# Linear attention with experts on one Trainium2 core: queries and keys by two levels of Strassen's algorithm, attention stages among their products

## The chip, the cores and the metric

The kernel runs on one core of a Trainium2 chip. The metric is the time of one execution on the device in microseconds; lower is better. The core has a matrix engine (TensorE, PE in the profile; its weight loads are PEld), a vector engine (VectorE, DVE), an engine for activations and copies (ScalarE, ACT), a general engine (GpSimd, POOL) and a queue that issues the DMAs (SyncE, SP). Each engine runs its instructions in the order in which they stand; a wait at the head of an engine holds everything behind it.

## What is computed

One layer, all of it in float32, on 1024 tokens (2 batches of 512) of width 512. The tokens are normalised; 32 heads of width 128 do linear attention with a decay per head, in blocks; the result is gated, normalised and projected back; a router with 8 experts of rank 16 and a base matrix are added.

```python
xn  = layernorm(x)
qkv = silu(xn @ qkv_w.T)                       # 32 heads x (q, k, v) x 128
for each block:                                # state kv: 128x128 per head and batch
    scores = (q @ k.T) * diag_decay
    out    = scores @ v + (q * q_decay) @ kv
    kv     = kv * block_decay + (k * k_decay).T @ v
gate = sigmoid(xn @ gate_w.T)
attn = gate * (norm_w * rms_normalised(out)) @ out_w.T
ffn  = xn @ W_base.T + b_base + sum over the top 2 of 8 experts of B_e (A_e xn) * 2 * weight
return x + attn + ffn
```

## The kernel before

**Setup.** The eight tiles of 128 tokens are loaded, normalised and transposed to xnT (one tile for each batch). The router's and the experts' first products (ra) and the base product (seeded banks, sent to DRAM as x_base) follow. The four blocks of xnT (feature half by batch) and their Strassen sums xsum are the outer level's seven operands xo[1..7]; for each, four inner sums xt[q] are made.

**Values and gates, two levels of Strassen's algorithm** (Winograd's form, seven products in place of eight, at each level). There are eight sets: values and gates of eight heads each, in turn. A set is seven rounds, one for each outer product q; a round is seven inner products of two matmuls with 256 columns (inner_product, L304 for values, L307 for gates). GpSimd prepares the weights' sums two rounds ahead (encode, L178 the outer and L192 to L195 the inner sums). The sums of products are made partly in PSUM: SLOTS gives the order of a round, (0,1), (0,5), (0,2), (1,7), (0,6), (0,3), (1,4), where the first number says whether the product belongs to this round or to the one before. Product 1 goes to bank pa; ScalarE copies pa to pb (L368) while product 5 runs; product 2 is added onto pa; product 6 onto pb; ScalarE copies pb to pd (L375); products 7 and 4 are added onto pd, 3 onto pc. VectorE takes y from pc and w from pb (L361) and adds the rest (L342, L346, L354). The outer level's sums x1, u2, u3, u4 are kept in SBUF (sum, 4 buffers). The round q=7 gives two outer results and so has the most vector work. pa and pc come from three "fr" banks, pb and pd from four seeded banks. Results pass through silu or tanh (L320, L322) and go to DRAM (v_kept, gate_kept). Routing (route, transpose_experts) stands among the first rounds.

**Queries, keys and attention.** Then the pools change. For each head a unit makes q and k for both batches with one level: seven products of two matmuls with 512 columns (product, L482), with the sums of the weights on GpSimd (load_unit, L127 to L130), sums of products on VectorE (L497) and silu on ScalarE (L493); four "ch" banks. Between the products of pair p+1 stand the attention stages of pair p. An item is one head and batch, 64 in all. Its stages (attend): k is transposed in squares of 32 on VectorE (L543) and goes to DRAM and back as kt (L545, L550); scores (8 instructions on TensorE) and their mask (L558), qd on GpSimd (L561); kd on ScalarE from kt (L566); the blocks' states (6 instructions) and their recurrence on VectorE (L574, L576); the output pa (14 instructions), its square sq on ScalarE (L589) added to ssq on GpSimd (L590), and gT on VectorE (L592), which goes to DRAM (g_kept). Attention has two "sc" and two "at" banks. The experts' second products stand in the same loop (experts, eight times). From the last two pairs on, the out weights (load_out_w, scaled on ScalarE, L636) and the first gated inputs are loaded, and twelve early out products stand between the last attention stages.

**Out projection.** One level of Strassen over token half f and head pair p (out_product, L666, 256 columns); operands are summed on VectorE (L647 to L650) and GpSimd (L654 to L657); the results are scaled, added to x_back and stored.

The order on each engine is made by a scheduler from the order of the program and a model of readiness; buffers are given out from each pool's free slots.

Of the kernel before, what the change touches and what calls it, by code (L numbers as in the profile page):

```python
# [22 lines left out]

# [12 lines left out]
ALU = mybir.AluOpType  # L36
# [23 lines left out]
def attn_moe_kernel(ctx: ExitStack, tc: tile.TileContext, x, qk_w, v_w, gate_w, out_w, norm_w,  # L60
                    decay, base_w, base_b, router_a_w, lora_b, out):
    nc = tc.nc

    def pool(name, space=None, bufs=1):
        kw = {"space": space} if space is not None else {}
        return ctx.enter_context(tc.tile_pool(name=name, bufs=bufs, **kw))

    keep = pool("keep")
    dram = pool("dram", DRAM)
    wts = pool("wts")  # L70
    phase_a = ctx.enter_context(ExitStack())
    ps = phase_a.enter_context(tc.tile_pool(name="ps_a", bufs=1, space=PSUM))
    seeded = [ps.tile([P, 512], F32, tag=f"sd{i}", name=f"sd{i}") for i in range(4)]
    banks = {"fr": 3, "ra": 1}
# [3 lines left out]

    def mm(o, lhsT, rhs, start, stop):
        nc.tensor.matmul(o, lhsT, rhs, start=start, stop=stop)  # L80

# [4 lines left out]
    hT = keep.tile([P, NT, P], F32, tag="hT", name="hT")  # L86
    nw = keep.tile([P, H], F32, tag="nw", name="nw")
    xnT = [wts.tile([P, KC, S], F32, tag=f"xnT{b}", name=f"xnT{b}") for b in range(B)]
    xsum = [wts.tile([P, 2, S], F32, tag=f"xsum{i}", name=f"xsum{i}") for i in range(4)]
# [5 lines left out]
    x_kept, x_base = (dram.tile([P, NT, HID], F32, tag=n, name=n) for n in ("x_kept", "x_base"))  # L95

# [20 lines left out]
    units, masks = {}, {}  # L117
    wts_of = [wts, wts]

    def load_unit(i):  # L120

        where = wts_of[i // 2 % 2]
        w = where.tile([P, 2, KC, P], F32, tag="w", name="w", bufs=2)
        nc.sync.dma_start(w, qk_w[i])
        s = where.tile([P, 4, 2, P], F32, tag="ws", name="ws", bufs=2)
        a11, a12, a21, a22 = w[:, 0, 0:2], w[:, 0, 2:4], w[:, 1, 0:2], w[:, 1, 2:4]
        nc.gpsimd.tensor_tensor(s[:, 0], a21, a22, ALU.add)  # L127
        nc.gpsimd.tensor_tensor(s[:, 1], s[:, 0], a11, ALU.subtract)
        nc.gpsimd.tensor_tensor(s[:, 2], a11, a21, ALU.subtract)
        nc.gpsimd.tensor_tensor(s[:, 3], a12, s[:, 1], ALU.subtract)  # L130
        units[i] = w, s

    def load_pair(p):

        if p >= NP:
            return
        for j in range(2):
            m = wts.tile([P, 2, P], F32, tag="mask", name="mask", bufs=4)

            nc.sync.dma_start(m[:, 0, :], decay[2 * p + j][:, :P])  # L140
            nc.sync.dma_start(m[:, 1, :], decay[2 * p + j][P - 1, P : 2 * P].partition_broadcast(P))
            masks[2 * p + j] = m

    aw = phase_a.enter_context(tc.tile_pool(name="aw", bufs=1))
    NSET = 2 * (NG // 2)
    raws, sums2, operand = {}, {}, {}

    def load_set(n):  # L150
        s_, kind = divmod(n, 2)
        r = raws[n] = aw.tile([P, 2, HG * KC * P], F32, tag="raw", name="raw", bufs=2)
        for u in range(2):
            if kind == 0:
                nc.sync.dma_start(r[:, u].rearrange("p (k f) -> p k f", k=KC), v_w[2 * s_ + u])
            else:
                for f in range(HG):
                    nc.sync.dma_start(r[:, u, f * KC * P : (f + 1) * KC * P].rearrange("p (k d) -> p k d", k=KC),
                                      gate_w[8 * s_ + 4 * u + f])

    def raw_block(n, fo, ko):


        if n % 2 == 0:
            v = raws[n].rearrange("p u (ko ki fo y) -> p u ko ki fo y", ko=2, ki=2, fo=2)
            return v[:, :, ko, :, fo, :]
        v = raws[n].rearrange("p u (fo fi ko y) -> p u fo fi ko y", fo=2, fi=2, ko=2)
        return v[:, :, fo, :, ko, :]

    def inner(n, block, fi, ki):  # L170
        x_, y_ = (ki, fi) if n % 2 == 0 else (fi, ki)
        return block[:, :, x_, y_ * P : (y_ + 1) * P]

    def encode(n, q):

        def outer(k, a, b, op):
            t = sums2[n, k] = aw.tile([P, 2, 2, 256], F32, tag="s", name="s", bufs=4)
            nc.gpsimd.tensor_tensor(t, a, b, op)  # L178

        if q == 6:  # L180
            outer(1, raw_block(n, 1, 0), raw_block(n, 1, 1), ALU.add)
            outer(2, sums2[n, 1], raw_block(n, 0, 0), ALU.subtract)
        elif q == 7:
            outer(3, raw_block(n, 0, 0), raw_block(n, 1, 0), ALU.subtract)
        elif q == 3:
            outer(4, raw_block(n, 0, 1), sums2[n, 2], ALU.subtract)
        block = {1: lambda: raw_block(n, 0, 0), 2: lambda: raw_block(n, 0, 1), 3: lambda: sums2[n, 4],
                 4: lambda: raw_block(n, 1, 1), 5: lambda: sums2[n, 1], 6: lambda: sums2[n, 2],
                 7: lambda: sums2[n, 3]}[q]()
# [9 lines left out]
    for n in range(NSET):  # L199
        start = {0: [(0, 1), (1, 1), (0, 6)], 1: [(1, 6), (0, 4)]}.get(n, [(n, 1), (n - 1, 4), (n, 6)])  # L200
        rounds += start + [(n, q) for q in (2, 5, 7, 3)]
# [3 lines left out]
    lg = aw.tile([P, NT, NE], F32, tag="lg", name="lg")  # L205
    hl = aw.tile([P, NT, NE, R], F32, tag="hl", name="hl")
    xt = [aw.tile([P, 4, S // 2], F32, tag=f"xt{q}", name=f"xt{q}") for q in range(1, 8)]
    with tc.tile_pool(name="setup", bufs=1) as sp:
# [5 lines left out]
        for t in range(NT):  # L214
            nc.sync.dma_start(x_sb[t], x[t * P : (t + 1) * P, :])
            if t == 2:
                nc.sync.dma_start(wra, router_a_w)
        nc.sync.dma_start(wbase, base_w)
        load_set(0)
        nc.sync.dma_start(nw, norm_w)  # L220
        load_set(1)
# [4 lines left out]
        def base(t):  # L226

            b, tt = divmod(t, TB)
            bp = seeded[t % 4]
            for c in range(KC):  # L230
                mm(bp, xnT[b][:, c, tt * P : (tt + 1) * P], wbase[:, c, :], c == 0, c == KC - 1)
            o = sp.tile([P, HID], F32, tag="based", name="based", bufs=3)
            nc.scalar.copy(o, bp)
            nc.sync.dma_start(x_base[:, t, :], o)


        stats = sp.tile([P, NT, 6], F32, tag="stats", name="stats")
        mv = sp.tile([P, NT, 2], F32, tag="mv", name="mv")
        for g, ts in enumerate(((0,), (1, 2), (3, 4, 5), (6, 7))):
# [4 lines left out]
            for i, t in enumerate(ts):  # L244
                b, tt = divmod(t, TB)
                xn = sp.tile([P, HID], F32, tag="xn", name="xn", bufs=4)
# [3 lines left out]
                for c in range(KC):  # L250
                    nc.tensor.transpose(tp[:, c * P : (c + 1) * P], xn[:, c * P : (c + 1) * P], ident)
                nc.scalar.copy(xnT[b][:, :, tt * P : (tt + 1) * P],
                               tp.rearrange("p (c s) -> p c s", c=KC))
                ra = bank("ra")
                for c in range(KC):
                    mm(ra[:, : NE + ER], xnT[b][:, c, tt * P : (tt + 1) * P], wra[:, c, :],
                       c == 0, c == KC - 1)
                nc.scalar.copy(lg[:, t, :], ra[:, :NE])
# [17 lines left out]
        for t in range(NT):  # L276
            base(t)
# [565 lines left out]
```

## Time and profile before

| what | value |
|---|---|
| median of 3 runs | 1201.85 us (1201.69 to 1202.39) |
| the profiled execution: time, span | 1200.23 us, 1198.4 us |
| granted TensorE clock | 1.0 in all slices |
| setup and base products | 0 to 52 us, TensorE busy 42.0 us |
| values and gates | 52 to about 405 us |
| queries, keys, attention | about 407 to 1009 us |
| out projection | about 1009 to 1198 us |
| L482, both operands from sums | x384, mean of one 593 ns, busy 179.9 us |
| L307 sd<-xt,e | x224, mean of one 379 ns, busy 55.0 us |
| POOL L590 ssq, L561 qd | mean 1279 ns, 1009 ns |
| ACT L566 kd, L589 sq | mean 612 ns, 593 ns |
| DVE L592 gT, L558 scores, L543 squares | mean 688 ns, 685 ns, 572 ns |
| DMA k_kept, kt, wo (time to landing) | 2.4 us, 2.7 us, 6.7 us |

How to read it: "busy" counts the time in which at least one instruction of the group runs. Matmuls overlap (the next one starts while the last still drains), so the mean of one is longer than its pitch. A matmul in float32 appears as two instructions. "Idle before, releaser" says what ended an engine's wait. The windows give the busy time of each engine in a stretch.

### The profile page before, as it was taken

Reading aid. Unit: us, or ns where it says so; the run is one execution under the profiler, and the core shown is the slowest. Engines: PE = TensorE matmul, PEld = TensorE weight load, DVE = VectorE, ACT = ScalarE, POOL = GpSimd, SP = SyncE. Lnnn points to the kernel's source line nnn. Section 1 sums busy time; section 2 is a strip of 40 time slices with the busy share of each in tenths; the row PEclk is TensorE's granted clock in tenths of the full one; section 3 lists DMA queues with packets and bytes.
Section 4 is the critical chain, followed back from the end, with each engine's and each line's share of the span. In section 5 each row is a group of like instructions: output and inputs, shape, how many; then the busy total and the mean of one; then the engine's idle time right before and its main releaser. Section 6 shows DMA issues by size and latency. Waiting matters only on the chain.

```text
span 1198.4 us, 15747 instructions
## 1 busy us (share of the span) xinstructions
PE 1179.0 (98%) x5352; PEld 863.1 (72%) x5352; DVE 660.0 (55%) x1158; ACT 375.2 (31%) x656; POOL 597.9 (50%) x670
## 2 busy tenths in 40 slices
PE   6999999999999999999999999999999999999998
PEld 5588888888888655666666666666666669888887
DVE  8777676675776544445445454444445644436334
ACT  3244444544444422232222223223222332310000
POOL 4547775766765233343443444344434344655552
PEclk9999999999999999999999999999999999999999
DMA  7214445244342555655565656655555655933221
GB/s 289 89 45 139 152 150 176 97 159 167 106 160 95 187 170 169 184 159 184 166 195 176 183 175 186 187 158 173 178 160 174 199 169 165 329 123 124 88 88 53
DMA packets 152240, 189.58 MB, mean 158 GB/s; under 512 B 47072, under 2 KB 114656, under 8 KB 150880
## 3 DMA queue, kind: packets, MB, share of 16 engines
q1 hardware_dynamic: 152160, 188.57, 49.5%
q8 instruction: 43, 0.70, 0.3%
q14 instruction: 37, 0.30, 0.1%
HBM read 119.31 MB, written 69.21 MB: 157 GB/s over the span
## 4 chain that ended last, share of the span: by engine, by line
PE 91%; DVE 6%; ACT 1%; issue 1%; DMA 0%; SPq 0%; DVEq 0%; ACTq 0%
PE ps_ch L482 32%; PE ps_ch L666 9%; PE ps_at L80 9%; PE ps_sc L80 8%; PE ps_fr L307 7%; PE ps_fr L304 6%; PE sd L307 5%; PE ps_sc L666 5%; PE sd L304 4%; PE ps_at L666 2%; PE sd L80 2%; DVE sum L346 2%; DVE z L346 2%; PE ps_ra L80 1%; DVE c L354 1%
## 5 line engine op out<-in xcount | busy, mean ns | idle before, releaser
L482 PE MATMUL ps_ch<-xsum,ws 128*128 128x512 f32 x384 | 179.9, 593 | 0.0
L561 POOL TENSOR_TENSOR qd<-q,mask 128x384 f32<-128x384 f32 x64 | 64.6, 1009 | 166.9 <-PE ps_at L80 166.9
L482 PE MATMUL ps_ch<-xnT,w 128*128 128x512 f32 x256 | 120.5, 593 | 0.8 <-DVE z L346 0.8
L482 PEld LDWEIGHTS ps_ch<-xsum,ws 128*128 128x128 f32 x384 | 68.3, 191 | 62.6 <-issue 62.2
L80 PEld LDWEIGHTS ps_at<-scores,v 128*128 128x128 f32 x512 | 77.4, 192 | 28.0 <-issue 25.8
L592 DVE SCALAR_TENSOR_TENSOR gT<-gate,ps_at 128x512 f32<-128x512 f32 x64 | 44.0, 688 | 95.6 <-ACT sq L589 89.9
L497 DVE TENSOR_TENSOR c<-ps_ch,u 128x512 f32<-128x512 f32 x96 | 66.4, 691 | 49.6 <-PE ps_ch L482 49.3
L127 POOL TENSOR_TENSOR ws<-w 128x256 f32<-128x256 f32 x32 | 23.6, 738 | 135.4 <-DMA w<-in_qk_w 129.2
L666 PE MATMUL ps_ch<-wsum,gsum 128*128 128x256 f32 x384 | 89.1, 379 | 0.0
L80 PE MATMUL ps_at<-scores,v 128*128 128x128 f32 x512 | 88.4, 275 | 0.0
L80 PEld LDWEIGHTS ps_sc<-q,k 128*128 128x128 f32 x512 | 67.2, 192 | 29.3 <-issue 29.2
L590 POOL TENSOR_TENSOR ssq<-ssq,sq 128x512 f32<-128x512 f32 x62 | 79.3, 1279 | 11.2 <-ACT sq L589 11.2
L666 PEld LDWEIGHTS ps_ch<-wsum,gsum 128*128 128x128 f32 x384 | 72.3, 190 | 9.5
L493 ACT ACTIVATE k<-c 128x512 f32<-128x512 f32 x64 | 40.3, 630 | 117.8 <-DVE c L497 117.8
L80 PE MATMUL ps_at<-qd,state 128*128 128x128 f32 x384 | 74.2, 275 | 0.0
L80 PEld LDWEIGHTS ps_sc<-v,kd 128*128 128x128 f32 x384 | 52.8, 191 | 28.4 <-issue 27.5
L654 POOL TENSOR_TENSOR wsum<-wo 128x256 f32<-128x256 f32 x32 | 25.0, 782 | 91.8 <-PE ps_ch L666 37.4
L647 DVE TENSOR_TENSOR gsum<-gated 128x256 f32<-128x256 f32 x32 | 16.8, 526 | 97.2 <-PE ps_sc L666 74.6
L482 PEld LDWEIGHTS ps_ch<-xnT,w 128*128 128x128 f32 x256 | 44.0, 191 | 33.7 <-issue 32.3
L80 PE MATMUL ps_sc<-q,k 128*128 128x128 f32 x512 | 67.5, 275 | 0.0
L589 ACT ACTIVATE sq<-ps_at 128x512 f32<-128x512 f32 x62 | 36.8, 593 | 91.0 <-PE ps_at L80 87.1
L566 ACT ACTIVATE kd<-kt,mask 128x384 f32<-128x384 f32 x64 | 39.2, 612 | 72.7 <-PE ps_sc L80 28.8
(224 smaller groups left out, 2551.1 us busy)
## 6 DMA issues: line engine op xcount, KB each, us to landing
w<-in_qk_w SPq DMA_DIRECT2D x32, 512.0 KB, 4.6
v_kept<-z SPq DMA_DIRECT2D x64, 256.0 KB, 2.4
gate_kept<-z SPq DMA_DIRECT2D x64, 256.0 KB, 2.4
v<-v_kept SPq DMA_DIRECT2D x64, 256.0 KB, 2.9
gate<-gate_kept SPq DMA_DIRECT2D x64, 256.0 KB, 2.9
g_kept<-gT SPq DMA_DIRECT2D x64, 256.0 KB, 3.2
gated<-g_kept SPq DMA_DIRECT2D x32, 512.0 KB, 3.8
k_kept<-squares SPq DMA_DIRECT2D x64, 192.0 KB, 2.4
```

Source lines behind the costliest of these rows:

```text
L80: nc.tensor.matmul(o, lhsT, rhs, start=start, stop=stop)
L304: nc.tensor.matmul(o.rearrange("p (g j d) -> p j g d", g=2, j=2)[:, u], x_[:, u * P : (u + 1) * P], a, start=first and u == 0, stop=True, ...
L307: nc.tensor.matmul(o[:, u * HB : (u + 1) * HB], a[:, u], x_, start=first and u == 0, stop=True, skip_group_check=True)
L346: nc.vector.tensor_tensor(o, v, outer_sums[n, src][:, ij], ALU.add)
L482: nc.tensor.matmul(o, a[:, c, :], b[:, c, :], start=first and c == 0, stop=c == 1, skip_group_check=True)
L493: nc.scalar.activation(to[n, b], c, AF.Silu)
L497: nc.vector.tensor_tensor(o, p, t, ALU.add)
L561: nc.gpsimd.tensor_tensor(qd, q[:, P:].rearrange("p (j n) -> p j n", j=TB - 1), mask[:, 1, :].unsqueeze(1).to_broadcast([P, TB - 1, P]), A ...
L566: nc.scalar.activation(kd.rearrange("p j (a d) -> p a j d", a=4), kt, AF.Copy, scale=mask[:, 0, P - 1 : P])
L590: nc.gpsimd.tensor_tensor(ssq[b], ssq[b], sq, ALU.add)
L592: nc.vector.scalar_tensor_tensor(gT, gate.pop((head, b)), 1.0, pa, ALU.add, ALU.mult)
L666: nc.tensor.matmul(sums[n][:, i * HO : (i + 1) * HO], l[:, i * P : (i + 1) * P], r, start=p == 0 and i == 0, stop=p == NP - 1, skip_group_ ...
```

## The change

Queries and keys become eight more sets of the same rounds as values and gates (kind 2; a set is four heads, its outer blocks are pairs of heads), each round again seven inner products with 256 columns. Their results stay in SBUF (ring "qk", four tiles of q and k of one item). When an item's q and k are complete, its attention begins: the transpose two slots later, kt six slots later, the other stages through a generator (stages) from which the loop takes one stage for each 49/24 slots. Items run in the order in which they are complete. What does not get a turn by the last round is done after it, with the early out products.

For this the pools are merged. Values and gates share the rings of the attention; weights come block by block (load_block, 5 tiles) in place of set by set; the sums have three buffers in place of four, u3 takes u2's place and the outer weight sum 4 takes 2's; PSUM is three seeded banks (pb always the first, pd the other two in turn), two "fr", two "sc" and one "at"; pa and pc share the two "fr" in the new sets, and pc has "sc" in the old ones. The router's result goes through DRAM (routed). The experts' products stand among the rounds of values and gates (from round 8, every third). Masks are loaded for each item in place of each head. The out weights of the first four pairs and the first three gated inputs are loaded when the rounds are over.

```diff
-    seeded = [ps.tile([P, 512], F32, tag=f"sd{i}", name=f"sd{i}") for i in range(4)]
-    banks = {"fr": 3, "ra": 1}
+    seeded = [ps.tile([P, 512], F32, tag=f"sd{i}", name=f"sd{i}") for i in range(3)]
+    banks = {"fr": 2, "sc": 2, "at": 1}
+    RING = {"qk": (2, 4), "v": (1, 5), "gate": (1, 4), "scores": (1, 3), "gT": (1, 2), "sq": (1, 1)}
...
-    NSET = 2 * (NG // 2)
+    VG = 2 * (NG // 2)
+    NSET = VG + NG
+    def kind(n):
+        return 2 if n >= VG else n % 2
+    def load_block(n, fo, ko):
+        t = blocks[n, fo, ko] = aw.tile([P, 2, 2, 256], F32, tag="raw", name="raw", bufs=5)
...
+    def place(n, fo, to, ij):
+        fi, ti = divmod(ij, 2)
+        if kind(n) < 2:
+            return ring("v")
+        item = 4 * (n - VG) + 2 * fo + fi, to
+        if item not in qk:
+            qk[item] = ring("qk", [P, 2, S])
+        return qk[item][:, :, ti * HB : (ti + 1) * HB]
...
+        elif ij in (1, 2):
+            complete((4 * (n - VG) + 2 * fo + fi, to))
...
         if i == 1:
-            st["pb"] = seed_bank()
+            st["pb"] = seeded[0]
             nc.scalar.copy(st["pb"], st["pa"])
...
-            st["pd"] = seed_bank()
+            st["pd"] = seeded[1 + r % 2]
...
+    def complete(item):
+        items.append(item)
+        g = running[len(items) - 1] = attend(*item)
+        ready[len(items) - 1] = now[0] + 4
+        later[now[0] + 2].append(g)
+        later[now[0] + 6].append(g)
...
+    def stages():
+        for i in range(ITEMS + 2):
+            if i < ITEMS:
+                while i not in ready or ready[i] > now[0]:
+                    yield None
+                next(running[i])
+            if 1 <= i <= ITEMS:
+                next(running[i - 1])
+            if i < ITEMS:
+                yield True
+            if 1 <= i <= ITEMS:
+                next(running[i - 1])
+                yield True
+            if i >= 2:
+                next(running[i - 2])
+                yield True
...
         if i in (1, 5):
-            st["pa" if i == 1 else "pc"] = bank("fr")
+            st["pa" if i == 1 else "pc"] = bank("fr" if kind(rounds[r][0]) == 2 or i == 1 else "sc")
         inner_product(...)
         after(r, i)
+        if items:
+            credit = min(credit + 24 / 49, 1.5)
+            if credit >= 1 and next(stage):
+                credit -= 1
...
-    def product(o, a, b, first):
-        for c in range(2):
-            nc.tensor.matmul(o, a[:, c, :], b[:, c, :], start=first and c == 0, stop=c == 1, ...)
-    def unit(n):
-        ...
-    def projections(p):
-        ...
...
+    for i in range(EARLY):
+        load_gated(0, i)
+        load_out_w(i)
+    load_out_w(EARLY)
+    left = 0
+    while True:
+        now[0] += 1
+        for g in later.pop(now[0], ()):
+            next(g)
+        s_ = next(stage, "end")
+        if s_ == "end":
+            break
+        if s_:
+            left += 1
+            if left == 3:
+                sums[0].update({1: bank("fr"), 6: bank("fr"), 5: seeded[0], 7: seeded[1]})
+                for i in range(EARLY):
+                    operands(0, i)
+            if left >= 5:
+                for e in [next(early, None)]:
+                    if e:
+                        out_product(0, *e, sums[0])
```

## The prediction

> **What bounds the kernel now.** I read the page's engine totals first, then its chain of waits, then the same chain in order of time.
>
> ```profile
> span 1198.4 us, 15747 instructions
> PE 1179.0 (98%) x5352; PEld 863.1 (72%) x5352; DVE 660.0 (55%) x1158; ACT 375.2 (31%) x656; POOL 597.9 (50%) x670
> ```
> ```profile
> 457.98 6.87 PE ps_ch L482 x16
> ...
> 1159.36 2.59 PE ps_ch L666 x12
> ...
> 1186.98 5.18 PE ps_sc L666 x24
> ```
>
> TensorE is busy 98% of the span and carries 91% of the chain; no other engine passes 55%. The chain gives the true pitch of a matmul (the group means overlap): 6.87/16 = 0.430 us with 512 columns, 5.18/24 = 0.2157 us with 256. So halving the columns halves the time, and a product of two levels pays nothing extra on TensorE. Each f32 product shows as two instructions.
>
> Next, how well each stage fills TensorE: the windows by stage, on five whole sets of values and gates (145.74 to 366.61), the change of stages, and the stage of queries, keys and attention.
>
> ```profile
> 145.74:366.61 220.87, 218.73 (x982) 182.49 (x981) 148.92 (x211) 100.44 (x180) 150.25 (x161) 1.00 0.43 143
> ...
> 398.00:410.00 12.00, 9.98 (x40) 7.08 (x39) 6.61 (x11) 5.92 (x10) 0.00 (x0) 1.00 0.65 205
> 410.00:984.00 574.00, 574.00 (x2561) 356.79 (x2560) 281.54 (x537) 169.79 (x284) 243.03 (x265) 1.00 0.58 177
> ```
>
> Columns after the length: busy time of PE, weight loads, DVE, ACT, POOL. One-level queries and keys run with no idle TensorE at all. The two-level rounds do not quite: a set of seven rounds takes 220.87/5 = 44.2 us, and its 7 x 28 instructions at 0.2157 us are 42.3. So the form that queries and keys now take loses 1.9 us a set. Where, the timeline shows, at the round q=7:
>
> ```profile
> 171.31 2.41 DVE L346 TENSOR_TENSOR sum<-c,sum 128x512 f32<-128x512 f32 x1
> 173.64 0.68 DVE L346 TENSOR_TENSOR z<-c,sum 128x512 f32<-128x512 f32 x1
> 174.24 0.68 DVE L361 TENSOR_TENSOR y<-ps_fr,sum 128x512 f32<-128x512 f32 x1
> ```
> ```profile
> 175.07 1.10 PE L304 MATMUL ps_fr<-e,xnT 128*128 128x256 f32 x4 [0.23 <-DVE y L361]
> ```
> ```profile
> 170.82 2.35 POOL L178 TENSOR_TENSOR s<-s,raw 128x1024 f32<-128x1024 f32 x1
> ```
>
> An add of two SBUF tiles that elsewhere takes 0.68 us takes 2.41 while GpSimd runs its 2.35 us add; VectorE falls behind, y comes late, TensorE waits.
>
> **The change, part by part.** *Products.* Out go 32 units of 14 products of 512 columns: 896 instructions x 0.430 = 385.3 us. In come 8 sets x 7 rounds x 14 products of 256 columns: 1568 x 0.2157 = 338.2. On the path: -47.1 us. The built order has the 784 added products of that form, so the change does what it says there. GpSimd loses the 128 adds of load_unit (0.74 us each) and gains the encoding, 30.05 us a set by the windows (150.25/5); VectorE and ScalarE trade the unit's adds and copies for a round's.
>
> *Loads of the other engines.* A set now goes with 8 items of attention. TensorE: an item is 28 instructions; the timeline has 8 of them in 0.89 us, 0.111 each, so 3.11 us, and a set is 42.3 + 24.9 = 67.2 us. VectorE: 148.92/5 = 29.8 us for the rounds, and per item gT 0.688, scores 0.685, transpose 0.572, state 0.278 + 2 x 0.285, together 2.79: 29.8 + 22.3 = 52.1 us (78%). GpSimd: 30.05 + 8 x (1.009 + 1.279) = 48.4 (72%). ScalarE: 100.44/5 + 8 x (0.612 + 0.593) = 29.7 (44%). None becomes the bound on average, so what costs is lateness inside a set.
>
> *Lateness of the rounds.* A round's copy pb<-pa (0.575 us) must finish while TensorE runs one slot (0.863 us). In half of the gaps an attention stage now stands between products, which lengthens the cover. But in the two rounds around q=7 VectorE has some 11.8 us of work without a break (170.1 to 181.9 in the trace); with 2 x 8/7 items it has 11.8 + 6.4 = 18.2 us in two rounds of 9.6, about no slack. The bounds: 0 if the attention hides everything, 5 us a set if the waits of gT for sq (89.9 us over 64 items, 1.4 each) are also paid for the 2.3 items in these rounds, 1.9 + 3.2. I take 1.9, the value of the same rounds in this trace.
>
> *A wait that moves.* ScalarE's kd waits for kt to come back from DRAM, by the waits:
>
> ```profile
> ACT kd L566 <- DMA kt<-k_kept: 24.8, 18, 3.2
> ...
> ACT kd L566 <- DMA mask<-in_decay: 12.2, 8, 2.1
> ACT kd L566 <- DMA w<-in_qk_w: 6.6, 3, 2.9
> ```
>
> These 43.6 us (0.68 an item) cost nothing now: behind kd stand silu and copies with four ch banks in reserve. Afterwards pb<-pa stands behind it, and the next product but one waits for that. The distance from the transpose to the loading of kt also falls, from one item (about 9.1 us) to four slots with half a stage each (4 x (0.863 + 0.53) = 5.6 us), against 2.4 us for the write and 2.7 for the read. Bounds: 0, or all 0.68 x 8 = 5.5 us a set. The urgent copy comes once in 9.6 us and 26 waits of 1.7 us stand over it a fifth of the time, so I take 0.6. Banks are scarcer too: pa and pc have two between them (before three for the rounds), attention's at one (before two). A bank's next use is at least two slots and a stage, 2.8 us, after its last, and its reader takes 0.69: 0.25 us a set, bounds 0 and 0.9 (one late reader of 0.69 and a slot's gap). Together 2.75 us a set, 22.0 us for eight.
>
> *The rule of the port.* That a VectorE add of two SBUF operands and a GpSimd add exclude each other is in the row of 2.41 us; its mean excess is (1.38 - 0.69) + (0.98 - 0.69) = 0.98 us for each of two pairs a set, which is already inside the 1.9. The Trainium skill, SBUF — State Buffer, section "Who interferes with whom", says that the later of the two is blocked for the whole of the other's instruction, and this speaks against the change, since qd and ssq add GpSimd reads there. By it, in the worst case, four adds a set each wait a whole 2.4 us, 9.6 us in place of 1.9 to 2.0: 62 us more in eight sets, and the sum would be near 1240; by the row it stays as above.
>
> *The seam and the end.* At 398 to 410 TensorE idles 2.0 us where the stages change; the rounds run through: -2.0. At the other end twelve of the 192 attention stages are left when the rounds run out (24 stages to 49 slots, starting three rounds late). The first four pairs of out weights and three of g are loaded only then, seven DMAs of 512 KB, where the kernel before spread them over two pairs of heads. In the built order 45 attention matmuls (10.0 us) stand after the last round, ahead of the first out product, which needs 6.7 us for the weight's landing and 0.71 for its scaling; after it each wsum takes GpSimd 4 x 0.77 us. Bounds: 0, or 11 us (3.67 MB at the 329 GB/s of the page's fastest slice); I take 3, since the weights' adds come about as fast as TensorE uses them.
>
> *Costed at nothing.* The trip of routing through DRAM and the blockwise loads of weights: hidden by the 26 us in which TensorE multiplies by wbase and by the two rounds of lead; uncovered, the trip costs 4.3 us (an x load's landing). The experts among the gates' rounds: 8 x 2.55 us more for GpSimd, which is busy 30 of 44 us there; uncovered up to 2.5 us each. Twice as many mask loads (SyncE's queue, ahead of kt): 0.77 us an item of issue on a queue whose waits are for free buffers. Out products after the stages: unchanged.
>
> Sum: -47.1 + 22.0 + 3.0 - 2.0 = -24.1 us on the profiled span of 1198.4, or 1174.3. The median of the runs shown is 1201.85, 3.45 above the span; less 24.1 it is **1178 us**.
>
> **The rivals.** *The attention hides the rounds' lateness* (1 us a set at most, 2 at the end): -47.1 + 8 + 2 - 2 = -39, **1163**. For it: idle-free TensorE from 410 to 984, where the attention already stands among products. Against: those had four banks and no copy on the path.
> *VectorE sets the pace of the heavy rounds*: 5 us a set, 40 + 3 - 2 - 47.1 = -6, **1196**. For it 18.2 us of work in 19.2; against, waits vanish when VectorE is the late one.
> *Slower: ScalarE blocked by kt.* If every item's kd waits the 1.7 us that 26 of 64 wait now, and half of it reaches TensorE through pb<-pa, that is 64 x 0.85 = 54 us: **1232**. It decides from 24.1/64 = 0.38 us an item beyond my sum. For it: the shorter distance, and one in-order queue. Against: kd still stands at least four slots behind kt.
>
> **How the numbers follow.** Forecast (1168 to 1190) 0.45; hidden 0.25; VectorE 0.15, of it 0.03 within 0.2% (2.4 us, about what a measurement here can tell from no change); ScalarE 0.15. So faster 0.82, same 0.03, slower 0.15. The range 1157 to 1203 leaves out the best of the second case and most of the last.
>
> **What would show it.** Right: about 67 + 3 us a set in the new stage, matmuls at 0.2157 us, short TensorE waits for y, z and pb<-pa near q=7. Hidden: sets of 68 us. VectorE: TensorE idle behind VectorE in the heavy rounds, VectorE gapless. ScalarE: kd waiting for kt, TensorE idle until pb<-pa just after. The end: how long TensorE idles before the first out product. The prediction is wrong if a set takes over 73 us or the first stage lengthens.

## The result, and the profile after

The changed kernel takes 1257.93 us (median of 4 runs, 1254.14 to 1264.23); the kernel before took 1201.77 us beside it. The ratio is 1.0473, 95% interval 1.043 to 1.0516: it is slower, where 1178 us was predicted. The profiled execution took 1264.23 us, with a span of 1262.4.

The page's engine totals and slices of the changed kernel:

```profile
span 1262.4 us, 17952 instructions
...
PE 1177.9 (93%) x6024; PEld 1004.1 (80%) x6024; DVE 768.2 (61%) x1334; ACT 439.7 (35%) x780; POOL 742.9 (59%) x798
...
PE   6999999999999999999999997988978967999998
...
PEclk9999999999999999999999997998988998999999
```

TensorE is no longer 98% busy. No engine has taken its place; the holes lie in slices 25 to 34, where the granted clock dips too. Those slices are the later sets of queries and keys. Windows on sets 10, 13 and 15 (counted from the first set of values; busy time of PE, weight loads, DVE, ACT, POOL, then the clock) show it:

```profile
542.00:610.00 68.00, 66.32 (x407) 59.99 (x407) 47.73 (x85) 28.38 (x51) 46.26 (x48) 1.00 0.60 177
752.00:839.00 87.00, 76.43 (x416) 65.32 (x415) 49.02 (x90) 29.47 (x52) 47.75 (x48) 0.90 0.45 135
925.00:1029.00 104.00, 87.52 (x507) 76.48 (x506) 59.78 (x115) 32.71 (x58) 48.31 (x49) 0.92 0.46 135
```

The first and the second do the same work: DVE 48 and 49 us, ACT 28 and 29, POOL 46 and 48. One takes 68 us and the other 87.

A ledger, read from the starts of the products; "lost" is a stretch less its matmuls at full pitch (0.430 us for 512 columns, 0.215 for 256, 0.111 for 128). Sets 0 to 7 are values and gates, 8 to 15 queries and keys; the tail runs from the last round to the first matmul on ones, which begins the out projection's final sums.

| us | before | after |
|---|---|---|
| to the first round | 51.8 | 52.8 |
| sets 0 to 7 | 45.9 43.5 44.1 44.1 44.2 44.1 44.2 44.7, sum 355.0 | 46.7 48.4 47.7 46.2 45.0 44.3 44.3 44.3, sum 366.8 |
| lost in them | 17.1 | 21.9 |
| sets 8 to 15 | | 53.3 69.2 68.3 68.2 73.9 86.8 86.1 103.5 |
| lost in them | | 1.6 2.2 2.8 4.2 8.8 20.9 19.1 27.1 |
| tail | | 47.8, lost 18.1 |
| queries, keys, attention in all: time, work, lost | 605.6, 604.3, 1.3 | 657.2, 552.1, 105.0 |
| out | 186.1 | 185.7 |

So the products' saving is there: TensorE has 52.2 us less to do in the second stage. But 105 us are lost in place of 1.3, and they grow from set to set. Sets 9 to 11 took 69.2, 68.3 and 68.2 us, what the prediction gave a set (67.2 + 2.75). From set 12 on it breaks down.

Where, the timeline in set 14 shows:

```profile
843.59 0.60 ACT L530 ACTIVATE sq<-ps_at 128x512 f32<-128x512 f32 x1 [5.29 <-PE ps_at L89]
...
844.26 1.27 POOL L531 TENSOR_TENSOR ssq<-ssq,sq 128x512 f32<-128x512 f32 x1 [5.46 <-ACT sq L530]
...
845.49 2.34 POOL L155 TENSOR_TENSOR s<-s,raw 128x1024 f32<-128x1024 f32 x1
...
847.79 0.99 POOL L499 TENSOR_TENSOR qd<-qk,mask 128x384 f32<-128x384 f32 x1
...
848.82 0.69 DVE L345 TENSOR_TENSOR qk<-sd,y 128x512 f32<-128x512 f32 x1 [3.91 <-POOL qd L499]
...
849.56 1.91 PE L293 MATMUL sd<-xt,s 128*128 128x256 f32 x4 [3.47 <-DVE qk L345]
...
852.23 0.63 ACT L318 ACTIVATE qk<-qk 128x512 f32<-128x512 f32 x1 [2.06 <-DVE qk L349]
852.77 0.58 ACT L378 COPY sd<-sd 128x512 f32<-128x512 f32 x1
...
853.40 2.08 PE L293 MATMUL sd<-xt,e 128*128 128x256 f32 x4 [1.93 <-ACT sd L378]
```

This is a chain through all four engines. ScalarE's square has waited 5.29 us for TensorE's output stage, and GpSimd stands 5.46 us in ssq, waiting for that square. Behind ssq stand an outer sum of the encoding and qd. qd is the last reader of a q/k tile, and the ring has four, so VectorE may not write the next q until qd is done (3.91 us); TensorE's product waits for that add (3.47 us). Four matmul instructions take about 1.03 us at full clock; here they take 1.91 and 2.08, at half. The second of them had waited for a copy on ScalarE, which stood behind a silu that waited 2.06 us for VectorE's next q/k add. The waits of the whole run (us in total, times, longest), first the longest of all, then one from ScalarE's list:

```profile
POOL ssq L531 <- ACT sq L530: 185.1, 47, 10.5
```
```profile
ACT kd L506 <- DMA kt<-k_kept: 3.6, 3, 1.9
```

The kernel before had 11.2 us of the first:

```profile
POOL ssq L590 <- ACT sq L589: 11.2, 9, 3.3
```

The second answers to the 24.8 us that kd waited for kt before: the rival that blamed kt is refuted.

The instructions on each engine are much the same in every set from 9 on, but their built order is not. TensorE's, one line a set, where a dot is a product, s a scores or states stage and each a one of the seven matmuls of an output stage:

```
set 9   ..s..aaaaaaa..s..s..aaaaaaa..s..s..aaaaaaa..s..s..aaaaaaa..s..s..aaaaaaa...s.s..aaaaaaa...s.s..aaaaaaa....s.s..aaaaaaa..s
set 11  ...s.aaaaaa.sa......ssaaaaaaa....s.aa.saaaaa....s.aa.saaaaa.....s.aaaaaasa......saaaasaaa........saaaasaaa......
set 13  aasaaa......saaaaaasa.....saaaa.aasa.......ssaaaaaaa....s.aasaaaa.a....s.aa.saaaa.a...s.aaaasaaa.....saaaaaasa........
```

In set 9 the stages are spread over the products as the loop issues them. From set 11 on the scheduler puts two or three side by side, with up to eight products without one. GpSimd's order changes likewise: in sets 9 to 11 encodings and attention's adds take turns, from set 12 on two encodings stand behind three pairs of qd and ssq.

### The profile page after: what moved, and what is told of

It reads as the page before. It is cut to its first block, busy times and chain, and to the rows that moved or that the text cites. A ratio compares the mean times of both kernels' runs of the same rounds, so it can differ in the third digit from the quotient of the medians.

```text
span 1262.4 us, 17952 instructions
## 1 busy us (share of the span) xinstructions
PE 1177.9 (93%) x6024; PEld 1004.1 (80%) x6024; DVE 768.2 (61%) x1334; ACT 439.7 (35%) x780; POOL 742.9 (59%) x798
## 4 chain that ended last, share of the span: by engine, by line
PE 65%; DVE 9%; POOL 6%; issue 4%; DMA 3%; ACT 2%; SPq 2%; DVEq 0%; ACTq 0%; POOLq 0%
PE ps_fr L293 15%; PE sd L293 12%; PE ps_at L89 6%; PE ps_sc L89 6%; PE sd L652 6%; PE ps_fr L652 4%; PE ps_sc L652 4%; PE sd L290 4%; PE ps_sc L293 3%; PE ps_fr L290 3%; PE ps_sc L290 2%; DVE sum L349 2%; DVE v L349 2%; DVE qk L349 2%; POOL s L155 1%
## 5 line engine op out<-in xcount | busy, mean ns | idle before, releaser
L293 PE MATMUL sd<-xt,e 128*128 128x256 f32 x672 | 172.3, 385 | 6.0 <-ACT sd L378 5.8
L293 PEld LDWEIGHTS sd<-xt,e 128*128 128x128 f32 x672 | 125.7, 193 | 24.6 <-ACT sd L378 9.2
L318 ACT ACTIVATE qk<-qk 128x512 f32<-128x512 f32 x128 | 80.5, 630 | 152.0 <-DVE qk L349 90.4
L170 POOL TENSOR_TENSOR e<-s 128x256 f32<-128x256 f32 x64 | 46.7, 730 | 95.4 <-PE sd L293 70.5
L293 PE MATMUL ps_fr<-xsum,s 128*128 128x256 f32 x288 | 81.9, 406 | 12.0 <-DVE qk L349 11.8
L371 ACT COPY sd<-ps_fr 128x512 f32<-128x512 f32 x112 | 64.3, 574 | 77.4 <-PE ps_fr L293 48.3
L378 ACT COPY sd<-sd 128x512 f32<-128x512 f32 x112 | 64.4, 575 | 64.1 <-PE sd L293 47.5
L155 POOL TENSOR_TENSOR s<-raw 128x1024 f32<-128x1024 f32 x32 | 77.6, 2425 | 11.8 <-DMA raw<-in_qk_w 5.2
L89 PE MATMUL ps_at<-qd,state 128*128 128x128 f32 x384 | 76.8, 282 | 7.3 <-DVE state L516 6.2
L89 PEld LDWEIGHTS ps_at<-scores,v 128*128 128x128 f32 x512 | 77.2, 197 | 6.8 <-issue 2.5
L293 PEld LDWEIGHTS ps_fr<-xsum,s 128*128 128x128 f32 x288 | 54.2, 200 | 27.5 <-DVE qk L349 11.8
L89 PEld LDWEIGHTS ps_at<-qd,state 128*128 128x128 f32 x384 | 61.5, 196 | 11.0 <-DVE state L516 7.2
L499 POOL TENSOR_TENSOR qd<-qk,mask 128x384 f32<-128x384 f32 x64 | 65.9, 1035 | 7.0 <-ACT qk L318 2.5
L89 PE MATMUL ps_sc<-qk 128*128 128x128 f32 x512 | 69.5, 280 | 0.0
```

The source lines that it names most:

```text
L293: nc.tensor.matmul(o[:, u * HB : (u + 1) * HB], a[:, u], x_, start=first and u == 0, stop=True, skip_group_check=True)
L318: nc.scalar.activation(v, v, AF.Silu)
L371: nc.scalar.copy(st["pb"], st["pa"])
L378: nc.scalar.copy(st["pd"], st["pb"])
L499: nc.gpsimd.tensor_tensor(qd, q[:, P:].rearrange("p (j n) -> p j n", j=TB - 1), mask[:, 1, :].unsqueeze(1).to_broadcast([P, TB - 1, P]), A ...
```

## The experiments

Theory 1 is GpSimd's queue (1a: its order; 1b: its load), theory 2 that four q/k tiles are too few, theory 3 the loads at the end, theory 4 TensorE's order. All times are beside the kernel before at 1201 to 1203 us; one without a ratio or a number of runs is a single run, and the changed kernel's own four runs spread over 10 us.

**Breaking single links.** The first two runs move one add from GpSimd to VectorE:

```diff
-        nc.gpsimd.tensor_tensor(qd, q[:, P:]...                  # e1
+        nc.vector.tensor_tensor(qd, q[:, P:]...
-            nc.gpsimd.tensor_tensor(ssq[b], ssq[b], sq, ALU.add)  # e2
+            nc.vector.tensor_tensor(ssq[b], ssq[b], sq, ALU.add)
-    RING = {"qk": (2, 4), "v": (1, 5), ...                        # e3; e4 has qk 4, v 3; e8 is e1 and e3
+    RING = {"qk": (2, 5), "v": (1, 3), ...
```

> qd is made on VectorE instead of GpSimd; all else as in the changed kernel. Theory 1 (GpSimd's queue): VectorE's write of a new q/k tile waits 43 us in all for qd, which stands on GpSimd behind ssq and the weights' sums. With qd on VectorE that wait is gone, sets 12 to 14 (73.9, 86.8, 86.1 us) fall to about 69 as sets 9 to 11, the windows at half clock in them go too: 1205 to 1225 us. Theory 2 (four q/k tiles are too few, whoever reads them): VectorE then waits for the scores on TensorE instead, sets 12 to 14 stay above 80, 1245 to 1265 us. Theory 3 (weights come late: SyncE's queue and the adds): no change, 1250 to 1265 us.

Measured 1213.7 us, as theory 1 has it. Sets 12 to 15 fall to 65.1, 72.1, 72.4, 91.7.

> The sum of squares (ssq + sq) is made on VectorE; qd stays on GpSimd. Theory 1: GpSimd waits 185 us in all for sq at these adds, with qd and the weights' sums behind; without them qd comes when its item is ready, sets 12 to 14 about 70 us, 1210 to 1230 us; VectorE gets 62 x 0.7 us more. Theory 2 and theory 3: sets 12 to 14 stay above 80, 1245 to 1270 us.

Measured 1232.19 us, between the forecasts; these sets 68.2, 78.9, 79.3, 95.2.

> Five q/k tiles instead of four, the room for it from the ring of v (three instead of five). Theory 1: one more item of slack, about 8.5 us, covers most of the waits for qd: sets 12 to 14 about 70 to 75 us, 1210 to 1235 us. Theory 2: the same. Theory 3: no change in sets 12 to 14. If the ring of v itself is too short now, sets 1 to 7 get longer, as in the run with v alone at three.

Measured 1227.19 us; 73.5, 79.1, 79.4, 82.0.

> The control for the run with five q/k tiles: only the ring of v at three instead of five. All theories: not faster than the changed kernel, 1255 to 1285 us; what it adds in sets 0 to 7 is to be taken off the other run.

Measured 1252.16 us: beside this control the fifth tile is worth 25 us, and the shorter v ring costs nothing that these runs show.

> qd on VectorE and five q/k tiles (the v ring cut from 5 to 3) together. Alone they gave 1213.7 and 1227.2 (1252.2 for its control). If theory 1 and theory 2 name two causes that add up: 1190 us or less. If both relieve the same chain (a q/k tile comes free only after qd has read it): 1203 to 1214, sets 13 and 14 below 72 us and only set 15 and the tail left.

Measured 1222.2 us. They do not add up: with both, it is 8 us slower than qd on VectorE alone, above both expectations. Each of the single links (ssq, qd, tile) helps when it is broken, qd most. In the trace of the run with qd on VectorE TensorE's order is still bunched from set 12 on.

**The order.** GpSimd's encodings, qd and ssq are chained in the order in which the program emits them; nothing is added or taken away:

```diff
+    def pool_tt(*a):
+        ins = nc.gpsimd.tensor_tensor(*a)
+        if in_order:
+            tc.add_manual_dep(ins.ins, in_order[-1].ins.name, NO_SYNC, reason="order")
+        in_order.append(ins)
```

> Only the order of GpSimd's instructions is fixed: encodings, qd and ssq stand in the order in which the program emits them, the same in every set, instead of the order that the scheduler made (regular in sets 9 to 11, from set 12 on two encodings behind three pairs of qd and ssq). No work is added or removed. Theory 1a (the bunched order is what makes sets 12 to 15 long): they go back to about 68 to 72 us each (now 73.9, 86.8, 86.1, 103.5), and the kernel takes 1185 to 1205 us. Theory 1b (GpSimd is late because of its load and its waits, whatever the order): sets stay at 80 or more, the time within 15 us of 1258. Theory 2 (four q/k tiles): as 1b.

Measured 1201.61 us, 56 us less with the same instructions and the same loads. Three windows of this run, in sets 10, 13 and 15:

```profile
531.00:599.00 68.00, 66.95 (x412) 60.71 (x411) 47.02 (x86) 28.74 (x51) 45.58 (x47) 1.00 0.60 179
736.00:810.00 74.00, 70.71 (x422) 62.06 (x423) 48.78 (x92) 28.73 (x52) 47.57 (x48) 1.00 0.58 174
884.00:968.00 84.00, 78.27 (x476) 68.23 (x476) 56.89 (x111) 32.30 (x58) 50.02 (x50) 1.00 0.51 150
```

Theory 1b falls, and theory 2 with it as a cause of its own. Sets 12 to 15 are 71.7, 73.2, 74.3 and 83.8 us: the growth is small, but not gone. The clock is full in these windows, and sets 5 to 7 take 43.2 in place of 44.3 us.

> As the pinned order, but the inner sums of an encoding are issued at the fifth slot of a round instead of the first, after the last product that reads the tile which they overwrite. Theory 1a: at least as good as the pinned order alone, 1180 to 1205 us, and GpSimd's waits of e for TensorE (sd) shrink below half of what the pinned order shows. Theory 1b and theory 2: within 15 us of 1258.

Measured 1202.85 us: where the inner sums stand within a round does not matter to the time. GpSimd's waits of e for TensorE fell from 88.0 to 61.6 us, not below half, and nothing came of it.

> The pinned order, and an item's two mask loads issued before its k_kept write instead of behind it. With the pinned order GpSimd still waited 106.6 us (28 times) in qd for its mask, whose load stands on SyncE behind a write that waits for VectorE (86.5 us, 26 times). Theory: that lateness makes sets 12 to 15 71.7, 73.2, 74.3 and 83.8 us; with the masks in time they fall to 67 to 70 (15: to 78), and the time to 1175 to 1190. Rival: qd is early anyhow (its reader stands two stages behind), nothing changes: 1198 to 1204, and the sets stay.

Measured 1204.15 us (ratio 1.0026, 1.0012 to 1.004); sets 12 to 15 take 71.3, 73.8, 73.7, 86.2. The rival holds. GpSimd's wait for masks was long (88.0 us left) and cost nothing.

> As the run with masks first, and the loads of the first out weights and gated tiles (seven DMAs of 512 KB) are issued one pair for each attention stage after the last round, instead of all of them ahead of the last items' k, v and gate loads. The stretch from the last round to the first matmul on the ones took 48.8 us for 29.7 of work with the pinned order. Theory (the big loads delay the last items' loads): 8 to 14 us less than the run with masks first. Rival (the last items are a chain of latency, and the weights then come later still): within 3 us of it or longer.

Measured 1206.79 us; the tail 50.9 us against 47.6. The rival holds again: the big loads are not what delays the last items. That these are a chain of latency fits, but this run does not show it by itself.

**The experts.**

> An expert's two loads are issued two rounds ahead of its adds. If the 11.8 us that the first sets take more than before come from GpSimd waiting for these loads with the encoding behind it, sets 0 to 4 go from 46.7, 48.4, 47.7, 46.2, 45.0 to about 44 to 45, and the time falls by 8 to 12 us, to about 1247. If the adds' own 2.55 us on a GpSimd busy 84% of the time are what is late, the sets stay within 3 us in total and the time at 1254 to 1262.

Measured 1259.92 us, sets 0 to 4 48.4, 49.2, 47.7, 46.2, 45.0: bringing the loads forward takes nothing off.

> As the run with masks first, with the experts left out: the eight token tiles' adds of bias, x and the expert product are not done, and the base product's result is copied on alone, so the output lacks them. It sizes the experts among the first rounds. If their adds on GpSimd are what lengthens sets 0 to 4: these fall from 46.7, 46.1, 46.2, 45.1, 43.8 to 43 to 44, 8 to 12 us in all. If they cost nothing, as the prediction put it: within 2 us of the run with masks first.

Measured 1193.26 us. Sets 0 to 7 take 347.3 in place of 357.3 us. But 6.9 of these 10.0 us are TensorE's own work: an expert's product is 2 instructions of 512 columns, 8 x 0.86. Only 3.1 are waits.

**The order in the kernel before.**

> The kernel before, with GpSimd's sums of values and gates fixed in the order in which the program emits them. With the pinned order the first stage of the changed kernel ran its later sets in 43.2 instead of 44.3 us. If that gain comes from the order and not from the change: sets 1 to 7 of the kernel before go from 44.1 to about 43.1, and it takes 1192 to 1196 us. If it does not: 1200 to 1203.

Measured 1194.89 us, ratio 0.9942 (0.9926 to 0.9959); sets 1 to 6 take 43.0 us. So some 6 us of what the fixed order gave have nothing to do with the change.

**TensorE's order.** The same chain of dependencies, on the products and attention's matmuls:

```diff
+    def pinned(engine, ins):
+        if engine in in_order:
+            tc.add_manual_dep(ins.ins, in_order[engine].ins.name, NO_SYNC, reason="order")
+        in_order[engine] = ins
...
-                nc.tensor.matmul(o[:, u * HB : (u + 1) * HB], a[:, u], x_, ...)
+                pinned("tensor", nc.tensor.matmul(o[:, u * HB : (u + 1) * HB], a[:, u], x_, ...))
```

> Only TensorE's order is fixed to the one in which the program emits products and attention stages; every other engine keeps the scheduler's order, made anew. In the changed kernel TensorE's built order spreads an item's three stages over the products in sets 8 to 10 and sets two or three stages side by side, with up to eight products without one between, from set 11 on. Theory 4 (the stages' bunching on TensorE is the root, GpSimd's bunched order and the late qd follow from it): sets 9 to 15 all take 67 to 70 us, the time is 1172 to 1190. Theory 1a (GpSimd's order alone): GpSimd's order changes little by this, the sets stay above 72, 1200 to 1240. Theory 2 (four tiles of q and k): above 1240.

Measured 1223.95 us, ratio 1.0179 (1.0161 to 1.0197). The growth is gone: sets 9 to 15 take 71.1, 76.0, 75.9, 77.2, 76.0, 75.7, 76.8, the tail 41.7 us. But they settle at 76, not 68: theory 4 is right about the growth and wrong about the size. Here GpSimd's order, left to the scheduler, no longer has two encodings behind three pairs of qd and ssq in sets 12 to 14, while in the run with GpSimd's order fixed TensorE's stayed bunched in them. So in these builds GpSimd's bunching goes with TensorE's, and not the other way round. Theory 1a's numbers for this run (1200 to 1240, sets above 72) came, its reason did not.

> TensorE's and GpSimd's order fixed together. Theory 4: the stage gains no more over TensorE alone than GpSimd's pinned order gains in the first eight sets (8 to 10 us): 1163 to 1180. Theory 1a: this is where sets 12 to 15 come down, 20 us or more below the run with TensorE alone.

Measured 1209.79 us, ratio 1.0067 (1.0042 to 1.0092): 14 us less, 11 of them in the first eight sets (357.1 against 368.6). Sets 10 to 14 still take 75.7 to 77.1, so GpSimd's order is not what holds them, and both forecasts (1163 to 1180; 20 us or more) missed. The waits name the next link, in TensorE's list of the run with both fixed:

```profile
PE ps_sc L93 <- ACT kd L518: 33.2, 23, 2.8
```

and ScalarE's timeline in the run with TensorE alone, with TensorE's product behind it:

```profile
699.11 0.63 ACT L330 ACTIVATE qk<-qk 128x512 f32<-128x512 f32 x1 [2.64 <-DVE qk L361]
699.65 0.60 ACT L518 ACTIVATE kd<-kt,mask 128x384 f32<-128x384 f32 x1
```
```profile
700.30 0.94 PE L93 MATMUL ps_sc<-v,kd 128*128 128x128 f32 x6 [1.19 <-ACT kd L518]
```

kd does not wait for kt. It stands behind a silu that waits 2.64 us for VectorE's add.

> As TensorE and GpSimd pinned, with the experts' adds of bias and x on VectorE instead of GpSimd. Leaving the experts out took 10.9 us off. If GpSimd's 2.55 us for two adds are that term: sets 0 to 4 fall to 43 to 45, 6 to 10 us less than the run with both pinned. If it is the loads or the port that both engines share: within 3 us of it.

Measured 1226.75 us, 17 more: sets 0 to 2 take 48.0, 52.5 and 48.5 us. VectorE is the worse place for these adds; neither expectation held.

**ScalarE's order.** TensorE's, GpSimd's and ScalarE's order fixed, and kd issued a stage earlier:

```diff
             if i < ITEMS:
                 next(running[i])
-            if 1 <= i <= ITEMS:
-                next(running[i - 1])
-            if i < ITEMS:
                 yield True
             if 1 <= i <= ITEMS:
                 next(running[i - 1])
                 yield True
+            if i < ITEMS:
+                next(running[i])
```

> TensorE's, GpSimd's and ScalarE's order fixed, and an item's kd issued one stage earlier (beside the output of the item two before, not beside the scores of the next item). With TensorE and GpSimd fixed, sets 10 to 14 took 75.8 us each, of them 8.7 lost, and what TensorE waited for was kd (33.2 us, 23 waits), which stands on ScalarE behind silu, which waits for VectorE's qk (127.7 us, 69 waits). Theory: ScalarE's order is the third queue that has to be right; the waits for kd go, sets 10 to 14 fall to 67 to 70 and the time to 1165 to 1185, below the kernel before. Rival: kd is late whatever stands ahead of it (its kt or VectorE), or ScalarE in emission order now makes pb and the copies late: 1200 to 1215.

Measured 1255.47 us, ratio 1.0439 (1.041 to 1.0467). Both theory and rival are right, in different stages: sets 9 to 15 take 69.7, 71.8, 69.8, 69.6, 71.7, 69.6, 72.5 us, as the theory has it, and sets 0 to 7 take 51.1 to 56.0 in place of 43 to 46. There the emitted order puts tanh and silu, which wait for VectorE, ahead of pb's copy:

```profile
206.64 1.23 ACT L330 ACTIVATE v<-v 128x512 f32<-128x512 f32 x2 [1.48 <-DVE v L357]
...
207.78 0.58 ACT L383 COPY sd<-ps_fr 128x512 f32<-128x512 f32 x1
...
208.41 2.07 PE L305 MATMUL ps_fr<-xnT,raw 128*128 128x256 f32 x4 [2.68 <-ACT sd L383]
```

> As the run with three engines fixed, and VectorE's order fixed too, so that all four engines go in the order in which the program emits. Theory: within 5 us of it, 1165 to 1190, since VectorE (78% of a set) has no long wait. Rival: an add that stands in emission order behind one whose product is not done holds VectorE up: 10 us or more above it.

Measured 1266.56 us, ratio 1.0545 (1.0523 to 1.0568): 11 us more, the rival by a little. Fixing VectorE's order too is of no use here.

**The parts together.** ScalarE's order is fixed from set 9 on only:

```diff
+        if engine == "scalar" and now[0] < 7 * 7 * (VG + 1):
+            return
```

> As the run with three engines fixed and kd one stage earlier, but ScalarE's order is fixed only from set 9 on; up to there it is the scheduler's. With ScalarE fixed from the start sets 0 to 7 took 51.1 to 56.0 us (waits for pb's copy behind tanh and silu) and sets 9 to 15 69.6 to 72.5. Theory: the first stage goes back to the 46.5, 46.1, 46.0, 45.1, 43.8, 43.2 x3 of the run with TensorE and GpSimd fixed, the second keeps its 69.6 to 72.5; with 40.3 for the tail and 182.4 for the out products the span is 1179 and the time 1176 to 1186, which is 1 to 2% below the kernel before. Rival: a set after the change of order pays back what was gained, or the first stage keeps ScalarE's lateness: above 1195.

Measured 1183.08 us (median of 6 runs, 1176.64 to 1187.77), ratio 0.9837 (0.9811 to 0.9862): as the theory has it. That is 1.6% faster than the kernel before, and 12 us below the kernel before with its own GpSimd order fixed. Its totals, then windows on sets 9, 11 and 14:

```profile
span 1184.5 us, 18100 instructions
...
PE 1146.0 (97%) x6024; PEld 998.4 (84%) x6024; DVE 758.1 (64%) x1334; ACT 439.0 (37%) x780; POOL 745.4 (63%) x798
```
```profile
466.00:536.00 70.00, 68.34 (x427) 62.65 (x426) 49.70 (x91) 29.16 (x53) 46.40 (x47) 1.00 0.61 177
605.00:677.00 72.00, 70.15 (x427) 64.07 (x427) 50.65 (x92) 29.30 (x52) 49.03 (x49) 0.98 0.61 178
820.00:890.00 70.00, 68.23 (x427) 62.54 (x426) 49.86 (x90) 29.12 (x52) 47.57 (x49) 1.00 0.61 177
```

Sets 9 to 15 take 69.4, 69.5, 71.3, 71.3, 72.7, 69.6, 72.5 us, the tail 39.4. Every set from 9 on now looks much like the others. What TensorE still waits for in this stage is mainly ScalarE's copy, 14.2 us in eight waits.

## Why the prediction was wrong

**The step that failed** is "None becomes the bound on average, so what costs is lateness inside a set", with its price of 2.75 us a set, 22.0 us for eight. It took the stages to stand in every set as the program emits them. In the scheduler's order they do not, and sets 8 to 15 lost 86.7 us, 75.9 of them in sets 12 to 15; sets 13 to 15 lost 19 to 27 us each, more than all the prediction's upper bounds for a set together (5 + 5.5 + 0.9). Both signs that it named for being wrong came: sets of over 73 us, and a longer first stage.

The averages were right: 47.7 us of VectorE, 46.3 of GpSimd and 28.4 of ScalarE in 68 us of set 10, against 52.1, 48.4 and 29.7 predicted. The price was near in the first sets, where the stages are still spread: sets 8 to 10 lost 1.6, 2.2 and 2.8 us. But the sum took this for eight sets alike, and it costed the order of the program where the engines run the scheduler's. In that order stages bunch from set 11 on. The built order was looked at for the number of products and for what stands after the last round; read set by set, it would have shown the bunching before any run.

That order is the cause is shown: with the same work on every engine the kernel takes 1201.61 us with GpSimd's order fixed, 1223.95 with TensorE's and, with three engines' fixed and kd a stage earlier, 1183.08. The program's order is not cheap by itself, though. With TensorE's and GpSimd's fixed to it sets 10 to 14 lost 8.7 to 10.1 us each, three times the price; only with ScalarE's order and kd's earlier stage did sets 8 to 15 lose 2.5, 2.4, 2.5, 4.2, 4.2, 5.6, 2.5 and 3.0, 26.9 us in all against 22.0. Not settled is how much of this last step is kd's earlier stage and how much ScalarE's fixed order, which were changed together.

**What the bound left out.** Lateness was bounded by VectorE's unbroken work and ScalarE's copies. GpSimd entered as a load of 48.4 us only. Its link to the path (ssq waits for a square, qd behind it holds a q/k tile, VectorE's add waits for the tile) was not seen; qd on VectorE took 44 us off. VectorE's work was also read as longer than it is: its rows from 170.1 us on have 10.3 us without a break and then 0.84 us of idle time, not 11.8 us unbroken.

**Products, -47.1 us.** Right. By count at full pitch the products fell from 385.3 to 337.1 us, 48.2. The second stage's work fell by 52.2: another 6.9 are the experts' products, now in the first stage, and 3.0 came back as out products that now stand in the tail.

**kd and kt, 0.6 us a set, and the slower rival (1232 us).** The releaser was wrong. kt waits shrank from 24.8 to 3.6 us, and in the changed kernel TensorE waited 8.8 us for kd; with TensorE's and GpSimd's order fixed kd did hold it up for 33 us, but behind silu. The price of a wait was misread as well: the three lines list 29 waits for 43.6 us, so 1.5 us each and not 1.7, which would put the rival at 1226.

**Scarcer banks, 0.25 us a set.** Right for attention's bank: TensorE waited 2.5 us for gT in the whole run. Wrong for the two "fr" banks, since the reader of a bank was taken at 0.69 us and never late. Here it is VectorE's q/k add, which had itself waited for qd (4.77 us before its longest), and TensorE's longest waits in total are for it:

```profile
PE ps_fr L293 <- DVE qk L349: 11.8, 4, 3.8
```

Whether a third "fr" bank would have taken these away was not tried.

**The port.** The worst case worked out from the Trainium skill, SBUF — State Buffer, section "Who interferes with whom", 1240 us, lies nearer to the result than the forecast, but by chance: the same adds on the same engines in another order take 1183 us. The trace's row was nearer to what collisions cost VectorE: in sets 8 to 15 of the changed kernel the 33 VectorE adds of two SBUF tiles took 15.4 us more than 0.69 us each, 1.9 us a set, where the row gives 1.96 and the worst case 9.6.

**The seam, -2.0 us.** Right: set 8 lost 1.6 us in all.

**The end, +3 us (0 to 11).** Mis-sized, and beyond its own bounds: the tail lost 18.1. The out weight cost 3.2 us, about what was taken for the whole end. TensorE's other waits there are for the last items' v (6.5), kd (1.2) and gT (2.1), and half clock cost some 3 us. Where TensorE's order was fixed and VectorE's was not, the tail lost 9.7 to 12.0; with VectorE's too it lost 3.4, but the set before it 9.4 in place of 3.1.

**Costed at nothing.** The first stage grew by 11.8 us: 6.9 is the experts' work, moved out of the second stage, and 4.8 (21.9 - 17.1) is more waiting. With GpSimd's order fixed, leaving the experts out took 3.1 us of waits away. Bringing their loads forward took away none.

**The clock.** Not in the prediction. It was at half in 58 us of the changed kernel, with TensorE busy for 47.6 of them, which is about 24 us lost. Some 19 of these fall in sets 12 to 15, a quarter of their loss. In the last experiment TensorE was busy for 19.6 us at half rate, about 10 us lost.

The ledger of the two profiled spans, 1198.4 to 1262.4: +1.0 before the first round, +11.8 in the first stage, -52.2 work and +103.7 loss in the second, -0.4 at the end: +63.9.

## What to carry to other kernels

When a scheduler orders the engines, a change that interleaves two streams has to be costed on the built order, period by period: if the same work stands in another order from one period to the next, the averages say little, and a chain through a small ring of buffers can grow from period to period. Fixing the order of one engine adds dependencies and no work, and tells order from load at once; but each stage needs its own, as ScalarE's emitted order (with kd earlier) gave 29 us in sets 9 to 15 and took 63 in sets 0 to 7.

## What the runs showed of the hardware that was not expected

The granted clock falls in whole steps of 3.41 us: in the changed kernel there are ten stretches of 3.41, 6.83 and 10.24 us at 0.5, nine of them soon after a wait of TensorE began. The tenth, at 1078.46, follows the eight matmuls of one column (sixteen instructions). All their starts and ends lie on one grid: those at 740.54, 761.02, 774.67 and 849.77 are 0, 6, 10 and 32 steps of 3.413 us from the first. The Trainium skill, TensorE: Matmul & The Clock Gate, section "What's actually happening", gives a free-running window of 3413 ns and half rate after an idle window. The grid agrees.

But the window need not be idle as a whole. Counted window by window on this grid, half rate followed in the changed kernel where a full-rate window had TensorE idle for 1.83 us or more, and not where it was idle for 1.74 or less, the window with the matmuls of one column aside. In the last experiment the two numbers are 1.85 and 1.77. Over all the runs here with half-rate stretches, every window with more than 2.0 us of idle time was followed by half rate, and those between 1.6 and 2.0 went either way. So what counts is how much of a wait falls into one window: a wait of 1.60 us (737.55 to 739.15) with a shorter one in the same window was followed by half rate, and one of 2.67 us (1028.94 to 1031.60) that lay across two windows was not. That is why a wait of about 2 us can cost more here than 2 us. The time of the last experiment's six runs goes with the mean granted clock: 1176.64 us at 1.000, 1187.77 at 0.992.
